# Queries and keys with the head ahead of the token: the layout between the projections and the score products

## The chip, the cores and the metric

The kernel runs on one core of a Trainium2 chip. The core has five engines with an instruction queue each: PE (TensorE, matrix products), DVE (VectorE), ACT (ScalarE), POOL (GpSimd) and SP (SyncE, which issues most of the DMAs here). Each engine works through its queue in order and waits at semaphores for the others. The metric is device time in microseconds (us) from one execution of the whole program; a single core runs, so it is that core's time. The time before is the median of three executions.

## What is computed

The reference is one pre-norm transformer layer in fp32 for 2048 tokens of width 1024. Its attention is not over the sequence: for every token, the 32 heads attend to each other.

```python
def _L0_attn_ref(hidden_states, wq, bq, wk, bk, wv, bv, wl, bl):
    ...
    q = (hidden_states @ wq.T + bq).reshape(B, S, H, D)
    k = (hidden_states @ wk.T + bk).reshape(B, S, H, D)
    v = (hidden_states @ wv.T + bv).reshape(B, S, H, D)
    ...
    scores = jnp.einsum('bshd,bstd->bsht', q, k) / np.sqrt(D).astype(np.float32)
    probs = jax.nn.softmax(scores, axis=-1)
    context = jnp.einsum('bsht,bstd->bshd', probs, v).reshape(B, S, E)
    return context
...
x = x + _L0_attn_ref(_layernorm(x, axis=-1), ...)
x = x + _L0_ffn_ref(_layernorm(x, axis=-1), ...)
```

H is 32 heads and D is 32 dimensions, so each token has a 32 x 32 score matrix. The feed-forward part is silu(x w1) * (x w2) times w3, with an inner width of 2752, where the three weights are first rounded to a 16-value code (NF4) with one scale for each block of 64.

## The kernel before

**Stages.** The kernel makes four passes one after the other. The query sweep, the key sweep and the value sweep each go over the 2048 tokens in 8 pairs of tiles; a tile is 128 tokens (P = 128), and a pair is put through a fast matrix product (`products`) with 7 block products in place of 8. Then comes the feed-forward part, which takes about two thirds of the time.

The query sweep normalises x, transposes it on PE for all three projections (`Inputs`), projects it to queries, brings them into their layout with `qk_T` and writes them to DRAM (`qD`). The key sweep loads the queries back (`ql`), projects the keys, brings them into the same layout with `qk_T` (`kd`), multiplies queries and keys (`scores`, in two parts of 64 products), takes the softmax (`softmax_T`) and writes the transposed probabilities to DRAM. The value sweep does the same with `v_T` and `context`, adds the residual and normalises again.

**Background.** Beside all of it, the feed-forward weights are quantised: for each block of 128 rows, ACT computes 15 steps `sg` (L211) and DVE folds each into `r` (L216). The code places these steps between the products by hand (`advance`, `flush`, `fill`). PE's order is exactly the one written; the order on the other engines is made by a scheduler when the program is built.

**The layout around the change.** A projected tile `c` holds 128 tokens on partitions and (head, dimension) along the free axis: `c[token, h*32 + d]`. For the score products, the dimension must be on partitions, since PE sums over partitions. DVE's transpose turns blocks of 32 x 32: for each group g of 32 tokens (partitions 32g to 32g+31) and each head it puts the dimension on the partition and the 32 tokens of the group along the free axis. Where these 32 tokens are written is a choice of the output's access pattern. Before, the tile `t` is (dimension; token, head): the 32 elements of a token, one for each head, lie next to each other, and a transpose writes every 32nd element.

The score product of token s in group g is a 32 x 32 x 32 product: its stationary operand is `qd[r, s, :]`, its moving operand `kd[r, s, :]`, with r the 32 partitions of group g. The four groups g use four row groups of PE's array, and the token's number modulo 4 selects the column group. [...]

`at` is the one score buffer in PSUM (four banks, `bufs=1`). The two DVE instructions that read it are the maximum (L543) and the subtraction (L545) in `softmax_T`.

**Lines that the steps touch.** L311 is the projection's matmul (`mm4`); L329 copies partial sums (g, s, u) on ACT, L346, L350 and L356 add them on DVE into the halves of the tiles `ce` and `co`, and L353 copies the last one into `ce`; L369 is the transpose in `qk_T`, L376 the one in `v_T`; L382 adds the bias; L390 is the score product; L543 to L557 are the softmax, with the exponential on ACT (L551) and the transpose of the probabilities (L557), which reads and writes consecutively; L522, L586 and L567 are the DMAs of queries and probabilities; L929 is the down projection of the feed-forward part.

Of the kernel before, what the change touches and what calls it, by code (L numbers as in the profile page):

```python
# [14 lines left out]
ALU = mybir.AluOpType  # L15
# [3 lines left out]
P = 128  # L19
# [3 lines left out]
D = 32  # L23
# [35 lines left out]
def preln_block_kernel(  # L59
# [14 lines left out]
    nc = tc.nc  # L74
# [291 lines left out]

    def qk_T(t, c, b):

        nc.vector.transpose(  # L369
            t.rearrange("p s h -> p h s"), c.rearrange("p (h d) -> p h d", d=D)  # L370
        )
        add_bias(t, b)

    def v_T(t, c, b):

        nc.vector.transpose(  # L376
            t.rearrange("p m d -> p d m"), c.rearrange("p (t d) -> p d t", d=D)
        )
        add_bias(t, b)

    def add_bias(t, b):
        nc.vector.tensor_tensor(t, t, b.unsqueeze(1).to_broadcast([P, 32, 32]), ALU.add)  # L382

    def scores(at, qd, kd, part):

        for s in range(16 * part, 16 * part + 16):
            c, s4 = s % 4, s // 4
            for g in range(4):
                r = slice(g * 32, (g + 1) * 32)
                nc.tensor.matmul(  # L390
                    at[c * 32 : (c + 1) * 32, g, s4 * 32 : (s4 + 1) * 32],
                    qd[r, s, :],
                    kd[r, s, :],
                    start=True,
                    stop=True,
                )
# [102 lines left out]
    for p in range(NP):  # L499
        more = p + 1 < NP  # L500
        now = nxt
        if more:
            load_x(2 * p + 2)
            load_x(2 * p + 3)
            nxt = Inputs(p + 1)

        def fill(n):
            if n in (7, 3):
                flush(1)
            if n == 5 and more:  # L510
                nxt.transposes(0)
                nxt.transposes(1)
            advance(0 if n == 5 else 1)

        cs = products(now.A, fill, (lambda name: None) if more else next_W("k"))
        flush(1)
        if more:
            nxt.finished()
        for j in range(2):
            t = work.tile([P, 32, NH], FP, tag="qd", name="qd", bufs=2)  # L520
            qk_T(t, cs[j], qb_sb)
            nc.sync.dma_start(qD[2 * p + j], t)  # L522
        now.finished_v()
        weight_chunk("kv"[p // 4], p % 4)
        advance(2)
        if p == NP - 2:
            first = load_A(opD, 0)
# [33 lines left out]
    def attend(i, qd, kd):  # L561

        at = ps_at.tile([P, 4, 512], FP, tag="at", name="sc")
        scores(at, qd, kd, 0)
        yield
        scores(at, qd, kd, 1)
        nc.sync.dma_start(pD[i], softmax_T(at))  # L567
        yield
# [13 lines left out]
    def load_tiles(src, p, tag, bufs):  # L582
        ts_ = []
        for j in range(2):
            t = work.tile([P, 32, NH], FP, tag=tag, name=tag, bufs=bufs)
            nc.sync.dma_start(t, src[2 * p + j])  # L586
            ts_.append(t)
        return ts_

    A = first  # L590
    for p in range(NP):
        nextA = load_A(opD, p + 1) if p + 1 < NP else load_A(opV, 0)
        qd = load_tiles(qD, p, "ql", 3)

        def fill(n):
            if n in (7, 2, 5, 4):
                part()
            advance(1)
            if n in (3, 5):
                flush(1)  # L600

        cs = products(A, fill, (lambda name: None) if p + 1 < NP else next_W("v"))
        flush(1)
        for j in range(2):
            t = work.tile([P, 32, NH], FP, tag="kd", name="kd", bufs=3)
            qk_T(t, cs[j], kb_sb)
            parts.append(attend(2 * p + j, qd[j], t))
        advance(2)
        A = nextA
# [70 lines left out]
    for p in range(NP):  # L680
# [26 lines left out]
        for j in range(2):  # L707
            t = work.tile([P, 32, D], FP, tag="vd", name="vd", bufs=3)
            v_T(t, cs[j], vb_sb)
            parts.append(gather(2 * p + j, pl[j], t))  # L710
# [320 lines left out]
```

## Time and profile before

| what | value |
|---|---|
| median of three executions | 2572.02 us (2563.67 to 2575.69) |
| the profiled execution | 2561.21 us, its span 2559.4 us |
| PE busy in the span | 2438.9 us (95%) |
| DVE busy | 2020.1 us (79%) |
| ACT busy | 1673.7 us (65%) |
| mean granted clock of PE | 0.985 of full speed |
| L369, transposes of queries and keys | 32, some 1.94 to 1.99 us each |
| L390, score products | 4096 matmul records, 42.2 us busy; 4096 weight loads, 38.0 us busy |

How to read it: a busy share is an average over stages with different limits, so the prediction reads each stage by itself. PE's matmuls overlap in its pipeline; a busy PE is not PE at its peak. PEld is PE's weight load, which overlaps its matmuls. The granted clock falls below 1.0 after PE has been idle for some time. In a list of waits, the name after the arrow is the instruction that released the waiting one, and "issue" means that the profile does not show what the engine waited for. A row of a group gives line, engine, operation, output and inputs, the shape and the count, then the busy time in us and the mean of one in ns, then the idle time before it.

### The profile page before, as it was taken

How to read it: one execution, taken by the hardware profiler on the slowest of the kernel's cores; microseconds unless marked ns; L12 is line 12 of the kernel's file. 1: busy time of each engine (PE TensorE's matmuls, PEld its weight loads, DVE VectorE, ACT ScalarE, POOL GpSimd, SP SyncE). 2: the span in 40 equal slices, each digit the busy share in tenths (PEclk: the TensorE clock that was granted, in tenths of full speed). 3: DMA queues.
4: the chain of work that ended last, by engine and by line, in shares of the span. 5: the costliest groups of instructions: out<-in, count | busy, mean ns of one | idle time of the engine just before them, and what ended most of it. 6: DMA issues, size and time to landing. Idle time of an engine off the chain costs nothing.

```text
span 2559.4 us, 36651 instructions
## 1 busy us (share of the span) xinstructions
PE 2438.9 (95%) x14160; PEld 1134.1 (44%) x14160; DVE 2020.1 (79%) x2240; ACT 1673.7 (65%) x3190; POOL 31.7 (1%) x72
## 2 busy tenths in 40 slices
PE   8899899999998999999999999999999999999998
PEld 4444444444444444444444444444444444444433
DVE  8999798888998588888888888889888897871222
ACT  4656554444654478979888898888987978861000
POOL 1000000000000000000000000000000000000000
PEclk9999999999999999999999999999999999999999
DMA  8778543656668673354644547335365253641474
GB/s 301 286 281 335 210 162 121 233 189 221 224 218 290 218 271 144 136 212 138 263 155 135 198 149 265 149 118 215 128 251 192 107 205 136 234 176 70 142 279 150
DMA packets 156848, 506.03 MB, mean 198 GB/s; under 512 B 13632, under 2 KB 67904, under 8 KB 136832
## 3 DMA queue, kind: packets, MB, share of 16 engines
q1 hardware_dynamic: 156096, 503.63, 54.3%
q8 instruction: 111, 1.82, 0.3%
q14 instruction: 65, 0.53, 0.1%
q10 hardware_dynamic: 576, 0.05, 0.0%
HBM read 317.77 MB, written 185.86 MB: 197 GB/s over the span
## 4 chain that ended last, share of the span: by engine, by line
PE 22%; DVE 21%; ACT 18%; issue 6%; DMA 1%; DVEq 0%; SPq 0%
DVE r L216 17%; PE z L311 9%; PE po L929 7%; ACT sg L211 7%; ACT wn L172 6%; PE q L311 3%; ACT r L172 3%; PE rr L311 2%; ACT wop L147 1%; DVE acc L950 1%; DMA acc<-x1d 1%; PE po L941 1%; DVE r L214 1%; DVE r L227 1%; PE ptw L146 0%
## 5 line engine op out<-in xcount | busy, mean ns | idle before, releaser
L211 ACT ACTIVATE sg<-wn 128x1024 f32<-128x1024 f32 (+1 forms) x975 | 1011.0, 1047 | 318.9 <-DVE r L216 272.4
L216 DVE SCALAR_TENSOR_TENSOR r<-sg,r 128x1024 f32<-128x1024 f32 (+1 forms) x910 | 1103.1, 1212 | 111.9 <-ACT sg L211 73.9
L929 PE MATMUL po<-w,h 128*128 128x512 f32 x1344 | 595.1, 597 | 17.0 <-DVE acc L950 13.8
L929 PEld LDWEIGHTS po<-w,h 128*128 128x128 f32 x1344 | 250.0, 190 | 336.5 <-issue 286.8
L311 PE MATMUL z<-xB,w 128*128 128x512 f32 x720 | 322.7, 597 | 13.7 <-DMA w<-wd 11.3
L311 PE MATMUL z<-xT,w 128*128 128x512 f32 x656 | 297.2, 596 | 2.0 <-ACT u L861 1.9
L311 PE MATMUL q<-xT,w 128*128 128x512 f32 x656 | 291.0, 592 | 0.0
L172 ACT ACTIVATE wn<-wn,rc 128x64 f32<-128x64 f32 x1032 | 270.1, 335 | 26.4 <-DVE rc L192 26.4
L311 PEld LDWEIGHTS z<-xB,w 128*128 128x128 f32 x720 | 134.5, 191 | 174.5 <-issue 164.3
L311 PE MATMUL z<-wB,A 128*128 128x512 f32 x384 | 188.6, 637 | 22.4 <-ACT u L329 22.4
L950 DVE TENSOR_TENSOR acc<-acc,po 128x512 f32<-128x512 f32 x192 | 129.7, 681 | 101.6 <-PE po L929 58.4
L311 PEld LDWEIGHTS q<-xT,w 128*128 128x128 f32 x656 | 123.6, 190 | 151.4 <-issue 149.5
L311 PE MATMUL z<-wT,A 128*128 128x512 f32 x384 | 181.3, 616 | 8.4 <-ACT u L329 6.4
L311 PEld LDWEIGHTS z<-xT,w 128*128 128x128 f32 x656 | 122.9, 191 | 149.8 <-issue 140.7
L311 PE MATMUL q<-wT,A 128*128 128x512 f32 x384 | 173.1, 593 | 3.0 <-DVE A L364 2.0
L172 ACT ACTIVATE r<-r,am 128x64 f32<-128x64 f32 x608 | 152.4, 338 | 27.9 <-DVE r L216 27.8
L311 PE MATMUL rr<-xB,w 128*128 128x512 f32 x328 | 150.0, 600 | 0.0
L184 DVE TENSOR_REDUCE am<-wn 128x16 f32<-128x1024 f32 (+1 forms) x65 | 78.3, 1204 | 59.4 <-ACT r L172 55.5
L311 PEld LDWEIGHTS z<-wB,A 128*128 128x128 f32 x384 | 75.0, 205 | 106.5 <-issue 79.3
L311 PEld LDWEIGHTS z<-wT,A 128*128 128x128 f32 x384 | 72.1, 195 | 91.0 <-issue 81.2
L311 PEld LDWEIGHTS q<-wT,A 128*128 128x128 f32 x384 | 71.8, 190 | 90.9 <-issue 84.2
L861 ACT COPY u<-z 128x512 f32<-128x512 f32 x41 | 23.5, 573 | 131.6 <-PE z L311 131.6
(104 smaller groups left out, 1798.4 us busy)
## 6 DMA issues: line engine op xcount, KB each, us to landing
w<-wd SPq DMA_DIRECT2D x41, 1280.0 KB, 6.9
acc<-x1d SPq DMA_DIRECT2D x96, 512.0 KB, 3.8
wd<-wop SPq DMA_DIRECT2D x21, 2048.0 KB, 7.0
x1d<-acc SPq DMA_DIRECT2D x80, 512.0 KB, 2.9
wn<-in_w_dram SPq DMA_DIRECT2D x63, 512.0 KB, 4.0
w<-wd SPq DMA_DIRECT2D x62, 512.0 KB, 4.1
xT<-xdT SPq DMA_DIRECT2D x28, 1024.0 KB, 7.2
xB<-xdB SPq DMA_DIRECT2D x24, 1024.0 KB, 5.2
```

The costliest lines, as they stand in the source:

```text
L147: nc.scalar.copy(o[:q, first + half], pt[:q])
L172: nc.scalar.mul(dst[:, ts(n, BLOCK)], src[:, ts(n, BLOCK)], by[:, n : n + 1])
L184: nc.vector.tensor_reduce(am[:, :nb], v.rearrange("p (b e) -> p b e", e=BLOCK), AX.X, ALU.max, apply_absolute_value=True,)
L211: nc.scalar.activation(t, v, AF.Copy, bias=EDGES[i], scale=BIG)
L214: nc.vector.tensor_scalar(r, t, code, -1.0, ALU.min, ALU.max)
L216: nc.vector.scalar_tensor_tensor(r, t, code, r, ALU.min, ALU.max)
L227: nc.vector.tensor_tensor(r3, r3, f, ALU.mult)
L311: nc.tensor.matmul(dst, w[:, k, :], xop[:, k, :], start=start and k == 0, stop=stop and k == 3, skip_group_check=True,)
L861: nc.scalar.copy(u2, self.z)
L929: nc.tensor.matmul(po, hs[c][j][:, ts(q, P)], w3T[c][:, ts(n, 512)], start=(c == g[0]), stop=(c == g[-1]), skip_group_check=True,)
L941: nc.tensor.matmul(po, hs[NFULL][r, ts(q, P)], w3T[NFULL][r, ts(n, 512)], start=False, stop=True, skip_group_check=True,)
L950: nc.vector.tensor_tensor(a[:, ts(n, 512)], a[:, ts(n, 512)], po, ALU.add)
```

## The change

Queries and keys are held as (dimension; head, token) in place of (dimension; token, head). The transposes of `qk_T` write the tile consecutively; the bias, one value for each head and dimension, is repeated along the last axis (the tokens) in place of the middle one; and the score products take token s as every 32nd element of the tile, in both operands. `add_bias` is now written out in its two places. The values' path keeps its layout, and the DMAs to and from DRAM move whole tiles as they did.

```diff
     def qk_T(t, c, b):

-        nc.vector.transpose(
-            t.rearrange("p s h -> p h s"), c.rearrange("p (h d) -> p h d", d=D)
-        )
-        add_bias(t, b)
+        nc.vector.transpose(t, c.rearrange("p (h d) -> p h d", d=D))
+        nc.vector.tensor_tensor(t, t, b.unsqueeze(2).to_broadcast([P, 32, 32]), ALU.add)

     def v_T(t, c, b):

         nc.vector.transpose(
             t.rearrange("p m d -> p d m"), c.rearrange("p (t d) -> p d t", d=D)
         )
-        add_bias(t, b)
-
-    def add_bias(t, b):
         nc.vector.tensor_tensor(t, t, b.unsqueeze(1).to_broadcast([P, 32, 32]), ALU.add)

     def scores(at, qd, kd, part):
...
                 nc.tensor.matmul(
                     at[c * 32 : (c + 1) * 32, g, s4 * 32 : (s4 + 1) * 32],
-                    qd[r, s, :],
-                    kd[r, s, :],
+                    qd[r, :, s],
+                    kd[r, :, s],
                     start=True,
                     stop=True,
                 )
```

## The prediction

> **What bounds the kernel now.** I read the busy time of the engines in four stretches first (query sweep after its start, key sweep, value sweep, feed-forward part; below I also call them stretches):
>
> ```profile
> core 0: us, PE busy (x) PEld busy (x) DVE busy (x) ACT busy (x) POOL busy (x), PEclk, DMA share, GB/s
> 35.00:283.00 248.00, 228.18 (x612) 106.79 (x611) 232.22 (x288) 164.05 (x333) 14.95 (x24) 0.97 0.78 291
> 283.00:553.00 270.00, 250.22 (x4582) 126.94 (x4581) 227.08 (x222) 126.73 (x244) 0.00 (x0) 0.97 0.47 175
> 553.00:850.00 297.00, 269.13 (x4715) 141.62 (x4714) 257.94 (x276) 150.44 (x295) 12.72 (x32) 0.96 0.71 236
> 850.00:2559.00 1709.00, 1666.30 (x4183) 744.48 (x4181) 1279.29 (x1426) 1223.62 (x2302) 0.00 (x0) 0.99 0.49 178
> ```
>
> Columns: stretch, its length, busy us of each engine, granted clock, DMA. The change touches the first two rows only. In the last, PE works 1666 of 1709 us, so whatever the sweeps gain or lose reaches the end almost whole. In the first, DVE is the fuller engine (232 of 248), in the second PE (250 of 270). Next, who waited for whom. PE and DVE in the query stretch:
>
> ```profile
> PE z L311 <- ACT u L329: 15.1, 7, 3.3
> PE pt L440 <- DVE xn L306: 3.7, 2, 2.8
> PE q L311 <- DVE co L356: 0.9, 2, 0.5
> ...
> DVE xn L306 <- POOL rs L108: 5.5, 10, 0.7
> DVE am L184 <- ACT r L172: 2.8, 1, 2.8
> ```
>
> and in the key stretch:
>
> ```profile
> PE sc L390 <- issue: 14.2, 5, 4.4
> PE sc L390 <- DVE kd L382: 5.6, 1, 5.6
> ...
> DVE ce L346 <- PE r L311: 17.7, 4, 5.3
> DVE mx L543 <- PE sc L390: 4.1, 6, 1.5
> ```
>
> Columns: total us, times, longest. In the query stretch DVE never waits for PE; PE waits for ACT's copy u, and ACT for DVE (36 waits of sg for r, 45.3 us): DVE sets the pace. In the key stretch each waits for the other. The timeline tells what stands behind "issue":
>
> ```profile
> 434.92 1.22 DVE L545 TENSOR_TENSOR pr<-sc,mx 128x1024 f32<-128x1024 f32 x1
> ...
> 436.24 1.41 PE L390 MATMUL sc<-kd,ql 32*32 32x32 f32 x128 [4.44 <-issue]
> ```
>
> (start, us, what.) The score products of the next tile begin when DVE has finished reading the last tile's scores out of the one score buffer: PE waits for DVE's queue.
>
> **The change, part by part.** Comparing the two builds, no instruction changes its place on any engine, the DMAs are the same whole tiles, and the queue of SP is untouched. Three things change their cost.
>
> *1. The transposes (L369).* These are the rows of the key stretch:
>
> ```profile
> L557 DVE STREAM_TRANSPOSE prT<-pr 128x1024 f32<-128x1024 f32 x16 | 19.8, 1240 | 0.3
> L555 DVE TENSOR_TENSOR pr<-pr,sm 128x1024 f32<-128x1024 f32 x16 | 19.5, 1218 | 0.3
> ...
> L382 DVE TENSOR_TENSOR kd<-kd,kb 128x1024 f32<-128x1024 f32 x16 | 19.2, 1203 | 0.1
> L369 DVE STREAM_TRANSPOSE kd<-ce 128x1024 f32<-128x1024 f32 x8 | 15.5, 1938 | 2.0 <-ACT ce L353 2.0
> ```
>
> L557 reads and writes consecutively, 1.240 us; L369 reads consecutively and writes every 32nd element, 1.938 us (1.98 in the query sweep). After the change L369 has L557's form: 16 x (1.98 - 1.24) = 11.8 us less DVE work in the query sweep, 16 x (1.938 - 1.240) = 11.2 in the key sweep.
>
> *2. The bias additions.* The bias is now repeated along the last axis, as the factor sm is in L555: 1.218 against 1.203 us, 32 x 0.015 = 0.5 us more. Nothing beside part 1.
>
> *3. The score products (L390).* Both operands, the stationary and the moving one, are now read every 32nd element. No PE row of the trace reads so; this is the open price. A half tile is 128 passes in 1.29 us:
>
> ```profile
> 426.88 1.29 PE L390 MATMUL sc<-kd,ql 32*32 32x32 f32 x128
> ...
> 428.10 3.70 PE L311 MATMUL z<-wT,A 128*128 128x512 f32 x8
> ```
>
> They run on four row groups of the array at once, so a group has 32 passes, 1290 / 32 = 40 ns each. L311 streams 512 elements in 429 ns (3.43 us for 8 in the undisturbed stretches), 0.84 ns per element, so 27 of the 40 ns are the 32 elements. There are 32 half tiles, so 32 x 32 = 1024 passes stand one behind the other: each ns on a pass is 1.02 us of PE.
> Low end: PE reads at any step for nothing, 0. High end: every element of load and stream costs the 1.938 us / 1024 = 1.89 ns of the strided transpose, and load and stream of a pass take turns: 2 x 32 x 1.89 = 121 ns in place of 27, +96 us. I take the nearest row, what the step adds per element on DVE: (1.938 - 1.240) us / 1024 = 0.68 ns, 32 x 0.68 = 22 ns on a pass, the weight load hidden beside the stream as now (PEld is busy half of PE's time): 22 ns x 1024 = +22 us of PE, a half tile of 2.0 us.
> The row of L369 against L557 shows that memory touched with a wide step costs more. [...]
>
> *The sum.* Query sweep: DVE sets the pace, so of 11.8 us most arrives; PE's own waits after the start are 15.1 + 3.7 + 0.9 = 19.7 us, enough room. As PE is 228 of 248 busy, it becomes the next bound at some places: I take two thirds, -8 (ends 0 and -15, the latter with half of the 3% of clock that idle PE lost, 7 us). Key sweep: PE has six waits, 19.8 us. Between a place where DVE waited for PE and such a wait stand about two transposes, so each shrinks by 1.4, the smallest (1.1) vanishes: -8 (ends 0 and -11). PE pays +22. The waits that are left, some 12 us, absorb little of this: DVE's own four long waits are for PE (17.7 us), so a late PE makes DVE late too; I take 3. Key sweep: 22 - 8 - 3 = +11. The value sweep's work is the same. Together -8 + 11 = +3 us.
>
> The profiled execution took 2561.2 us (span 2559.4 and 1.8 around it): it would become 2564. The median of the three runs shown is 2572.0, 10.8 above it (0.4%); the forecast in its terms is 2575.
>
> **Rivals.**
> *A. PE reads every 32nd element for nothing.* For: on PE fp32 asks for an element only each 0.84 ns, and four row groups already share the time of a pass, 13 of its 40 ns being no streaming. Against: the one engine whose step can be compared paid 56%. Then -8 - 8, and some 2 us of clock that is no longer lost to idle stretches: -18, 2554.
> [...]
> *C. The transposes don't get faster* because L557 owes its 1.24 us to its input rather than its order of writing: then only PE's part is left, 22 - 3 = +19, 2591. Against: L376 reads with a step as well and costs the same as L369, so the write decides.
>
> **How the numbers follow.** Forecast 0.38, A 0.27, B 0.30, C 0.05. What a measurement of this kernel can tell from no change is about 0.5%, 13 us. The forecast's own range is 2562 to 2592 (22 us of PE moved by 10 either way and 5 of the savings): a quarter of it lies beyond 2585, a twentieth below 2559. A is beyond 13 us in three cases of four, B nearly always, C in half. Faster 0.27 x 0.75 + 0.38 x 0.05 = 0.22; slower 0.30 x 0.95 + 0.38 x 0.25 + 0.05 x 0.5 = 0.40; same 0.38. The range goes from A's place, 2552, to a little above B's, 2628; the full high end (+96 us of PE) is left out.
>
> **What would show it.** L369 at 1.24 us, 32 times. [...] PE's waits in the query stretch fall from 19.7 to about 12 us, and the key sweep begins about 8 us earlier. [...] I am wrong if the half tile stays at 1.29 or passes 2.3 us, if the query stretch doesn't shorten with its transposes, or if the value sweep or the feed-forward part changes its length by more than 5 us, for nothing is changed there.

## The result, and the profile after

The changed kernel takes 2559.16 us in the median of 20 executions (2551.48 to 2564.3), the kernel before 2569.34 us in 20 (2560.44 to 2578.13). The ratio is 0.9961 with a 95% interval of 0.9951 to 0.9970: 10 us faster, where the forecast was 3 us slower.

The profiled execution of the changed kernel took 2564.3 us, the slowest of its 20; the profiled execution of before, 2561.2 us, lies below all but one of the 20 above. The two traces therefore show what the single steps did, but not the difference in time. These are the four stretches of the changed kernel, with the same columns and limits as before:

```profile
35.00:283.00 248.00, 231.32 (x737) 108.99 (x737) 229.17 (x295) 172.55 (x358) 14.94 (x24) 0.98 0.81 304
283.00:553.00 270.00, 264.44 (x4487) 141.70 (x4479) 216.32 (x220) 124.13 (x227) 0.00 (x0) 0.98 0.45 167
553.00:850.00 297.00, 267.40 (x4712) 140.81 (x4711) 253.97 (x272) 147.24 (x292) 12.67 (x32) 0.96 0.70 236
850.00:2559.00 1709.00, 1667.47 (x4176) 745.33 (x4174) 1279.19 (x1425) 1223.39 (x2302) 0.00 (x0) 0.99 0.49 177
```

In the key stretch PE is now busy 264 of 270 us instead of 250, and DVE 216 instead of 227. The limits are those of the kernel before; the key sweep now begins ahead of 283 us, so its first wait lies outside this row and more of the value sweep inside. Between the first and the last score product PE is busy 250.4 of 256.0 us, where it was 236.9 of 251.0. The groups of the changed lines (line, engine, operation, output and inputs, shape, count, then busy us, mean ns, and the idle time before):

```profile
L385 PE MATMUL sc<-kd,ql 32*32 32x32 f32 x4096 | 57.7, 263 | 11.1 <-DMA ql<-qD 5.6 <-issue 4.6 <-PE z L311 0.9
L385 PEld LDWEIGHTS sc<-kd,ql 32*32 32x32 f32 x4096 | 53.8, 168 | 35.8 <-issue 34.1 <-PE z L311 1.7
...
L369 DVE STREAM_TRANSPOSE kd<-ce 128x1024 f32<-128x1024 f32 x8 | 10.0, 1249 | 2.6 <-ACT ce L353 2.6
L369 DVE STREAM_TRANSPOSE kd<-co 128x1024 f32<-128x1024 f32 x8 | 10.0, 1244 | 0.1
L369 DVE STREAM_TRANSPOSE qd<-ce 128x1024 f32<-128x1024 f32 x8 | 9.9, 1240 | 1.4 <-ACT ce L353 1.4
L369 DVE STREAM_TRANSPOSE qd<-co 128x1024 f32<-128x1024 f32 x8 | 9.9, 1236 | 0.0
```

This is the group of the score products in the kernel before:

```profile
L390 PE MATMUL sc<-kd,ql 32*32 32x32 f32 x4096 | 42.2, 204 | 19.8 <-issue 14.2 <-DVE kd L382 5.6
```

The score products are now L385, and the bias additions of queries and keys L370. The transposes came down to 1.24 us, and the score products' matmuls went from 42.2 to 57.7 us of busy time. Both sides of the trade are there. On the timeline a call of `scores` shows the price for one half tile, 1.80 us in place of the 1.29 shown ahead of the prediction:

```profile
413.30 1.80 PE L385 MATMUL sc<-kd,ql 32*32 32x32 f32 x128
```

PE's idle time in front of score products fell from 19.8 to 11.1 us. And PE's waits in the query stretch, which were 15.1, 3.7 and 0.9 us:

```profile
PE z L311 <- ACT u L329: 8.4, 6, 1.9
PE pt L435 <- DVE xn L306: 2.6, 1, 2.6
```

They are now 11.0 us in place of 19.7: PE waits 8.7 us less in the query sweep.

### The profile page after: what moved, and what is told of

Read it like the earlier page. It is cut to its first block, busy times and chain, and to the rows that moved or that the text cites. A ratio compares the mean times of both kernels' runs of the same rounds, so it can differ in the third digit from the quotient of the medians.

```text
span 2562.5 us, 36651 instructions
## 1 busy us (share of the span) xinstructions
PE 2456.5 (96%) x14160; PEld 1151.3 (45%) x14160; DVE 2001.2 (78%) x2240; ACT 1674.9 (65%) x3190; POOL 31.6 (1%) x72
## 4 chain that ended last, share of the span: by engine, by line
PE 24%; DVE 20%; ACT 17%; issue 6%; DMA 1%; DVEq 0%; SPq 0%
DVE r L216 16%; PE z L311 9%; PE po L924 9%; ACT sg L211 7%; ACT wn L172 5%; PE q L311 3%; ACT r L172 3%; PE rr L311 2%; ACT wop L147 1%; DVE acc L945 1%; PE po L936 1%; PE ptw L146 1%; DVE r L214 1%; DVE r L227 0%; ACT u L856 0%
## 5 line engine op out<-in xcount | busy, mean ns | idle before, releaser
L216 DVE SCALAR_TENSOR_TENSOR r<-sg,r 128x1024 f32<-128x1024 f32 (+1 forms) x910 | 1104.2, 1213 | 113.5 <-ACT sg L211 75.5
L311 PE MATMUL z<-xB,w 128*128 128x512 f32 x720 | 323.3, 598 | 14.3 <-DMA w<-wd 12.0
L311 PE MATMUL z<-xT,w 128*128 128x512 f32 x656 | 297.2, 596 | 2.0 <-ACT u L856 1.9
L311 PE MATMUL q<-xT,w 128*128 128x512 f32 x656 | 291.0, 592 | 0.0
L311 PEld LDWEIGHTS z<-xB,w 128*128 128x128 f32 x720 | 134.9, 192 | 175.4 <-issue 165.0
L311 PE MATMUL z<-wB,A 128*128 128x512 f32 x384 | 186.3, 631 | 17.5 <-ACT u L329 17.3
L311 PEld LDWEIGHTS q<-xT,w 128*128 128x128 f32 x656 | 123.7, 190 | 151.3 <-issue 149.4
L311 PEld LDWEIGHTS z<-xT,w 128*128 128x128 f32 x656 | 123.0, 191 | 149.7 <-issue 140.6
L311 PE MATMUL z<-wT,A 128*128 128x512 f32 x384 | 181.4, 617 | 7.1 <-ACT u L329 4.5
L311 PE MATMUL q<-wT,A 128*128 128x512 f32 x384 | 173.1, 593 | 2.4 <-DVE A L364 1.5
L311 PE MATMUL rr<-xB,w 128*128 128x512 f32 x328 | 150.0, 601 | 0.0
L311 PEld LDWEIGHTS z<-wB,A 128*128 128x128 f32 x384 | 73.6, 201 | 100.9 <-issue 78.3
L311 PEld LDWEIGHTS z<-wT,A 128*128 128x128 f32 x384 | 72.4, 195 | 89.9 <-issue 81.7
L311 PEld LDWEIGHTS q<-wT,A 128*128 128x128 f32 x384 | 71.9, 190 | 90.0 <-issue 82.9
```

Of the source, the lines that this page charges most:

```text
L216: nc.vector.scalar_tensor_tensor(r, t, code, r, ALU.min, ALU.max)
L311: nc.tensor.matmul(dst, w[:, k, :], xop[:, k, :], start=start and k == 0, stop=stop and k == 3, skip_group_check=True,)
```

## The experiments

"Ratio" is always the time against the kernel before, run on the same chip beside it. "Half tile" is the 128 matmul records of one call of `scores`, two for each of its 64 products (4096 records in the profile for the kernel's 2048 products). The two theories that the first four runs were to tell apart concern PE's price (who pays for the step: the stationary operand, the moving one, or both) and where it ends up (on the path that sets the end, or hidden in PE's waits).

**1. The reading alone.** From the kernel before, only the operands change; the scores then mix heads and tokens.

```diff
-                    qd[r, s, :],
-                    kd[r, s, :],
+                    qd[r, :, s],
+                    kd[r, :, s],
```

> Layout and transposes as before, but the score products read both operands every 32nd element, so the scores mix heads and tokens. This is the price of the reading alone: a half tile of 1.79 us in place of 1.29, 32 x 0.50 = 16 us of PE. Theory of the critical path (PE sets the pace of the key sweep where it doesn't wait for DVE): +11 to +16 us (ratio 1.004 to 1.006), all in the key sweep. Rival (the extra PE time falls into PE's 20 us of waits in the key sweep and is hidden): 0 to +4 us (ratio 1.000 to 1.0015).

Measured: 2578.05 us, ratio 1.0025 (1.0013 to 1.0036), between the two theories. The group of the score products shows why:

```profile
L390 PE MATMUL sc<-kd,ql 32*32 32x32 f32 x4096 | 57.2, 263 | 12.8 <-issue 7.1 <-DMA ql<-qD 5.7
```

The busy time rose by 57.2 - 42.2 = 15.0 us, but the idle time in front of these products fell from 19.8 to 12.8. By this pair of traces 7.0 us of the price went into waits and 8.0 us lengthened the key sweep; against the second trace of before (run 10), whose idle time is 18.0 us, it is 5.2 and 9.9. The ratio gives 6.4 us (3.3 to 9.3). A price that arrives whole lies outside this interval, and so does full cover (a ratio of 1.000), while the upper end that the rival allowed itself (1.0015) lies just inside.

**2. The writing alone.** From the changed kernel, the operands are read as before; again the scores mix heads and tokens.

```diff
-                    qd[r, :, s],
-                    kd[r, :, s],
+                    qd[r, s, :],
+                    kd[r, s, :],
```

> Transposes write consecutively as in the changed kernel, but the score products read consecutive elements as before, so the scores mix heads and tokens. This is the gain of the writing alone: 23 us less DVE work. A half tile of 1.29 us. If the sum is additive with the reading alone and the whole change: -10 - 14 = about -24 us (ratio 0.9905 to 0.992): query sweep -11, key sweep -8 and more. Rival (DVE's gain counts in the query sweep alone, where DVE sets the pace): -11 us (ratio 0.996).

Measured: 2551.43 us, ratio 0.9921 (0.9906 to 0.9936), -20 us, some 4 us less than the additive sum. The rival's time (DVE counts in the query sweep alone, 0.996) lies outside the interval.

```profile
L385 PE MATMUL sc<-kd,ql 32*32 32x32 f32 x4096 | 42.2, 203 | 16.1 <-issue 10.1 <-DMA ql<-qD 6.0
L385 PEld LDWEIGHTS sc<-kd,ql 32*32 32x32 f32 x4096 | 37.9, 104 | 41.3 <-issue 40.8
```

With DVE faster and PE's price absent, the idle time in front of the score products is 16.1 us. Between this kernel and the changed one lies the reading alone: 15.5 us of price, of which 16.1 - 11.1 = 5.0 fall into waits, so 10.5 should arrive. The ratios differ by 0.0040, which is 10.3 us; that the two are so close is luck, since the intervals leave some 6 to 15 us. The reading alone and the writing alone add up to +6.4 - 20.3 = -14, against the measured -10 of both together. This is within the intervals, and on the side to be expected, as there is less waiting left for the price to fall into. The trace of the writing alone shows only a part of its -20 us: some 9 us at the first score product (282.5 us, against 291.1 and 291.8 in the two traces of before), and 1 to 3 us between the first and the last (247.7 us, against 251.0 and 248.6). Where the other 9 us sit, it doesn't show, so that they are DVE's gain in the key sweep is not shown either.

**3 and 4. One operand at a time.** The queries are the stationary operand, the keys the moving one, and each has its own layout. In the first run only the queries take the new one:

```diff
+    def old_T(t, c, b):
+
+        nc.vector.transpose(
+            t.rearrange("p s h -> p h s"), c.rearrange("p (h d) -> p h d", d=D)
+        )
+        nc.vector.tensor_tensor(t, t, b.unsqueeze(1).to_broadcast([P, 32, 32]), ALU.add)
...
-            qk_T(t, cs[j], kb_sb)
+            old_T(t, cs[j], kb_sb)
...
                     qd[r, :, s],
-                    kd[r, :, s],
+                    kd[r, s, :],
```

> Only the queries get the new layout: their transposes write consecutively and the stationary operand is read every 32nd element; the keys keep the old layout. Theory S (the moving operand's step costs, the weight load hides beside it): a half tile of score products stays at about 1.29 us, the query sweep gains about 11 us, the time is 11 us below the kernel before (ratio 0.996), as good as the whole change or better. Theory L (the stationary operand's step costs): a half tile of about 1.79 us, +16 us of PE in the key sweep, query sweep still -11, in sum near 0 (ratio 0.999 to 1.001). Theory B (each operand costs its half): a half tile of about 1.54 us, -11 + 6 = -5 us (ratio 0.998).

In the second only the keys (the queries use `old_T`, and the operands are `qd[r, s, :]` and `kd[r, :, s]`):

> Only the keys get the new layout: their transposes write consecutively and the moving operand is read every 32nd element; the queries keep the old layout. Theory S (the moving step costs): a half tile of about 1.79 us; the query sweep is unchanged, the key sweep gets +16 us of PE and -11 us of DVE, of which some 8 arrive: +5 to +8 us (ratio 1.002 to 1.003). Theory L (the stationary step costs): 1.29 us, -8 us (ratio 0.997). Theory B (half each): 1.54 us, about 0 (ratio 0.999 to 1.001).

Measured: queries alone 2559.88 us, ratio 0.9957 (0.9941 to 0.9972); keys alone 2565.69 us, ratio 0.9982 (0.9971 to 0.9993). The score products of the queries alone, and of the keys alone:

```profile
L392 PE MATMUL sc<-kd,ql 32*32 32x32 f32 x4096 | 50.2, 233 | 14.8 <-issue 9.6 <-DMA ql<-qD 5.3
L392 PEld LDWEIGHTS sc<-kd,ql 32*32 32x32 f32 x4096 | 46.4, 145 | 39.5 <-issue 33.4 <-DVE kd L377 6.1
```

```profile
L392 PE MATMUL sc<-kd,ql 32*32 32x32 f32 x4096 | 47.5, 229 | 14.9 <-issue 9.1 <-DMA ql<-qD 5.8
L392 PEld LDWEIGHTS sc<-kd,ql 32*32 32x32 f32 x4096 | 42.0, 104 | 40.3 <-issue 39.6
```

The stationary operand's step costs 50.2 - 42.2 = 8.0 us of PE, the moving one's 5.3; both together cost 15.0 to 15.5. So theory B is right on PE's side: each pays, and a weight load with a step isn't hidden beside the stream. The loads' mean, 105 ns before, grew to 145 ns with the queries alone and stayed at 104 with the keys alone. Both of its times were missed: -11 us for the queries alone, where it had -5, and -4.6 for the keys alone, where it had about 0. The price was again partly covered, as the idle time fell by 5.0 us with the queries alone and by 4.9 with the keys alone; in the latter DVE's faster transposes have a part in this.

**5 and 6. How far the step may go.** The kernel before with both operands read every 4th and every 2nd element of a smaller window (again a mix of heads and tokens):

```diff
+        q4, k4 = (
+            t.rearrange("p s h -> p (s h)").rearrange("p (b x k) -> p b x k", x=32, k=4)
+            for t in (qd, kd)
+        )
...
-                    qd[r, s, :],
-                    kd[r, s, :],
+                    q4[r, s // 4, :, s % 4],
+                    k4[r, s // 4, :, s % 4],
```

> The kernel before, but both operands of the score products are read every 4th element (a step of 16 bytes) out of a window of 128 elements, so the scores mix heads and tokens. It asks what the step costs, not the time. [...] Rival (it is the distance of 128 bytes, or the spread over 4 KB, that costs): near 1.29 us (busy 42 to 46 us).

> [...] Rival (any step but one costs the whole price): about 1.78 us (busy 57 us).

The groups with every 4th element, and with every 2nd:

```profile
L394 PE MATMUL sc<-kd,ql 32*32 32x32 f32 x4096 | 50.2, 239 | 17.6 <-issue 12.5 <-DMA ql<-qD 5.1
```

```profile
L394 PE MATMUL sc<-kd,ql 32*32 32x32 f32 x4096 | 42.6, 205 | 22.0 <-issue 16.6 <-DMA ql<-qD 5.4
```

Every 2nd element costs almost nothing (42.6 against 42.2 us), every 4th 8.0 us, every 32nd 15.0. So the price sets in between a step of 8 and one of 16 bytes; a step of 12 bytes was not run. Both rivals miss: the 50.2 us of every 4th element lie above the 42 to 46 of the one, the 42.6 of every 2nd far below the 57 of the other. About half of the price at 128 bytes comes on top of that at 16; these two runs don't show what from.

These two traces, one execution each (2572.45 and 2568.24 us, beside 2570.5 for the kernel before), also limit what was read from the first four. From the first to the last score product they took 258.4 us (every 4th) and 257.2 us (every 2nd, without a price), as long as the reading alone, 258.2, while the two traces of before took 251.0 and 248.6. The queries alone and run 8 below, which differ only in the value sweep's code, took 253.6 and 260.7. And of the 8.0 us of every 4th element only 2.2 fell into waits (19.8 to 17.6). So how a price divides between waits and path can't be read from one trace closer than by some us; the ratios of the first two runs are the firmer evidence.

**7. A padded tile.** The changed kernel with 36 elements for each head in place of 32:

```diff
-            t = work.tile([P, 32, NH], FP, tag="qd", name="qd", bufs=2)
+            t = work.tile([P, 32, 36], FP, tag="qd", name="qd", bufs=2)
+            nc.gpsimd.memset(t[:, :, 32:], 0.0)
...
-            t = work.tile([P, 32, NH], FP, tag="kd", name="kd", bufs=3)
+            t = work.tile([P, 32, 36], FP, tag="kd", name="kd", bufs=3)
```

(`qD` and the loaded tile `ql` likewise; `qk_T` works on the first 32 of each 36.)

> [...] POOL sets the four spare elements of the queries to zero, since whole tiles go to DRAM; the DMAs move an eighth more. The score products read every 36th element. [...] Rival (the distance alone costs): 1.79 us, 57 us busy, ratio 0.996 or worse by the padding's own work.

```profile
L386 PE MATMUL sc<-kd,ql 32*32 32x32 f32 x4096 | 50.5, 240 | 14.9 <-DMA ql<-qD 7.4 <-issue 7.4
```

A step of 144 bytes costs 8.3 us, about as one of 16 bytes does (8.0), and not the 15.5 of 128 bytes. So it isn't the distance: the longer step is the cheaper one, and why 128 bytes cost more, no run shows. The time, 2561.6 us and a ratio of 0.9965 (0.9953 to 0.9977), did not follow the lower price; it is where the rival had it. The first score products began at 284.9 us, some 4 us later than in the unpadded traces (281.6 and 279.2). But in the second padded kernel below, whose query sweep is the same code, they began at 280.9, so this delay is not a fixed price of the padding. Inside the key sweep the 7 us are missing too: from the first to the last score product the two padded traces took 254.2 and 254.4 us, the unpadded ones 256.0 and 253.9. In this time PE's products into z (L311) took 121.3 and 121.7 us in place of 118.3 and 116.6, at a granted clock of 0.96 in place of 0.98 and 0.99, and PE waited 7.4 and 7.2 us in place of 5.5 and 5.3. In the trace of before, after PE's 4.44 us of idle time that end at 436.24 us, the clock was 0.71 from 436 to 438 us, 0.50 to 440, 0.94 to 442 and 1.00 to 444; why it was lower in the padded traces, no run here shows.

**8 and 9. Towards a faster kernel.** The queries alone, and in the value sweep the context products' operands exchanged, so that the transpose of the context writes consecutively:

```diff
-                        prT[r, m, :],
                         vd[r, m, :],
+                        prT[r, m, :],
...
-            cx.rearrange("p (h d) -> p d h", d=D),
-            at[:, :, 0:256].rearrange("p c (s d) -> p d s c", d=D),
+            cx.rearrange("p (h d) -> p h d", d=D),
+            at[:, :, 0:256].rearrange("p c (s h) -> p h s c", h=NH),
```

> Only the queries get the new layout, and in the value sweep the two operands of the context products change places: the values become stationary, the probabilities moving, both still read consecutively. The context then lies as (dimension; head) in the score buffer, and the transpose that brings it back (16 of 1.97 us) writes consecutively: 16 x 0.73 = 11.7 us less DVE work in the value sweep, at no price on PE (a half tile of context products stays at 1.29 us). Theory (PE's waits for ACT's copies in the value sweep, 13.7 us, come from DVE's queue): another -5 to -10 us beside the -11 of the queries alone: ratio 0.992 to 0.994. Rival (the value sweep is set by PE, DMA and the loads of the feed-forward part): no more than the queries alone, 0.9957.

```profile
L406 PE MATMUL cx<-pl,vd x4096: 184/191/255, 558.2 to 825.7; 32*32 32x32 f32 x196
L622 DVE STREAM_TRANSPOSE cx<-cx x16: 1240/1244/1251, 566.8 to 826.5; 128x1024 f32<-128x1024 f32 x16
```

(Count, then the shortest, median and longest in ns, first and last start.) The transposes fell from a median of 1974 ns in the kernel before to 1244 at no price on PE, whose median stayed at 191 ns. From the last score product to the last context product this run took 287.3 us, against 292.0 with the queries alone. The time is 2556.33 us, ratio 0.9945 (0.9931 to 0.9959): some 3 us below the queries alone and not the 5 to 10 expected, and the intervals overlap. The same exchange on the padded kernel:

> The padded kernel, and the context products' operands changed over as in the run with the queries alone: 11.7 us less DVE work in the value sweep. There this gave the stretch from the end of the score products to the end of the context products 287.3 us in place of 292. Theory: -4 to -5 us beside the padded kernel (ratio 0.992 to 0.993 if the padding helps, 0.994 to 0.995 if not). Rival (the value sweep's gain is lost again in the feed-forward part): the padded kernel's ratio.

2558.59 us, ratio 0.9954 (0.9942 to 0.9967): 3 us again, below what was expected, with overlapping intervals. The queries alone with the exchanged operands have the lowest ratio of all kernels that leave the scores unmixed, though against the changed kernel it isn't clear of the measurement.

**10 and 11. Second traces.** Both kernels unchanged:

> The kernel before, unchanged, for a second trace: it tells how far the places of the sweeps differ from one execution to the next. The first score products of the first trace began at 291.1 us and the last at 542.1 us. Theory (the sweeps repeat within 2 us, and what differs between executions is the feed-forward part): 290 to 293 and 541 to 545 us. Rival (the first trace was a lucky one from the start): both later by 4 us or more.

> The changed kernel, unchanged, for a second trace: the first score products began at 281.6 us in the first one, the last ended at 537.9. Theory (the query sweep gains all of its 11.8 us of DVE work, less about 2): begin at 280 to 283 us, end at 534 to 540 us.

In the second trace of before the score products ran from 291.8 to 540.4 us, where expected for the start and 0.6 us before it for the end. In the second one of the changed kernel they ran from 279.2 to 533.1, each about 1 us before what was expected. These lines give the first and last start in the first trace of before and in the two of the changed kernel:

```profile
L390 PE MATMUL sc<-kd,ql x4096: 184/209/258, 291.1 to 542.1; 32*32 32x32 f32 x196
```

```profile
L385 PE MATMUL sc<-kd,ql x4096: 208/263/323, 281.6 to 537.6; 32*32 32x32 f32 x196
```

```profile
L385 PE MATMUL sc<-kd,ql x4096: 209/263/323, 279.2 to 533.1; 32*32 32x32 f32 x196
```

The four traces with the new layout for the queries and no padding or exchange (both traces of the changed kernel, the queries alone, the writing alone) begin at 281.6, 279.2, 281.1 and 282.5 us, mean 281.1. Six without it (both of before, the keys alone, the reading alone, every 4th, every 2nd) begin at 291.1, 291.8, 292.0, 292.7, 291.7 and 291.4, mean 291.8. The query sweep's gain is 10.7 us. (The queries alone with the exchanged operands, whose query sweep is the same code as that of the queries alone, began at 277.7; with it the gain would be 11.4.)

## Why the prediction was wrong

The forecast was -8 for the query sweep, +22 on PE for the reading, -8 and -3 in the key sweep; in sum +3, while the kernel became 10 us faster. Its structure held: two costs that lie in different sweeps, DVE setting the pace of the first. The step that failed by most is PE's price: +22 us, from a row of DVE and with the weight load hidden, where +15.5 was measured and the load's step is not hidden. Two smaller terms were also put too far towards slower (the query sweep by 2.7 us, what the waits absorb by some 2), and one the other way (DVE's gain in the key sweep, by 4.3). With these the sum is -4; where the other 6 us of the measured -10 sit stays open.

*The transposes* were right: 1.24 to 1.25 us against the 1.24 forecast, and the additions 1.21 to 1.23 us. (L376, which reads and writes with a step, took 1.97 and 1.99 us in the trace of before.)

*The query sweep:* I took two thirds of DVE's 11.8 us, "as PE ... becomes the next bound at some places". Measured: 10.7 us, nine tenths. PE had waited 19.7 us there, DVE never for PE, and the profile gave no row for the third that I withheld: after the change PE still waits 11.0 us there.

*PE's price:* the step added 0.47 ns per element (15.5 us over 1024 passes of 32), not DVE's 0.68: a half tile of about 1.79 us in place of my 2.0, +15.5 instead of +22. The row taken was of another engine and of a write, and this size failed. The overlap failed besides: I had the load "hidden beside the stream as now", while the stationary operand alone costs 8.0 us, more than the moving one's 5.3. Rival A, which needed 1.29 us for a half tile, falls. That load and stream take turns, from which rival B has its chance of 0.30 and the range its upper end of 2628 us, no run shows; the runs showed prices for the two operands that about add up (8.0 and 5.3 alone, 15.0 to 15.5 together), and a half tile below the 2.3 us that the prediction set as a bound (1.29 us and 32 us more over 32 half tiles, 13 us beyond the savings of 8 + 8 + 3). The change's own price lies between A's and mine.

*What the waits absorb:* I let the remaining waits absorb 3 of 22 us, because "a late PE makes DVE late too". With the reading alone the ratio lets 3.3 to 9.3 of 15.0 us arrive, so more than that vanished. Between the writing alone and the change the traces give 5.0 of 15.5, which is the case that the sum needed: 2 us more than mine, and not clear of the differences between traces. The two longest of DVE's waits for PE in the key sweep of the changed kernel are:

```profile
DVE ce L346 <- PE r L311: 24.8, 5, 7.0
...
DVE mx L538 <- PE sc L385: 7.3, 6, 2.4
```

My reason was right in the second line: the maximum that reads the score buffer waited 7.3 us for PE in place of 4.1, also with the reading alone (7.3), and 4.0 with the writing alone. The first line, 17.7 before, doesn't show it, since it is 21.8 with the writing alone, where PE pays nothing. The timeline suggests why more than 3 us vanished all the same: the wait for the one score buffer that is shown ahead of the prediction ends with DVE's subtraction (434.92 us), and a quantising step (L216, 433.79 us) stands just ahead of it in DVE's queue. PE's extra time may fall into such waits first; no run isolates this.

*The key sweep's gain from DVE* was over-estimated: with the writing alone PE's idle time before score products fell by 3.7 us (19.8 to 16.1), where I had 8. From busy and idle time of the score products, the key sweep's change is +15.5 - 8.7 = +6.8 us, where I had +11. With -10.7 that makes -4 us at the end of the key sweep. In the traces, the last score products start 542.1 and 540.4 us after the start before the change, and 537.6 and 533.1 us after it: 5.9 us earlier in the mean. The key sweep itself, from the first to the last score product, grew by 5.2 us, from 251.0 and 248.6 to 256.0 and 253.9; beside the 6.8 above, PE's products into z (L311) took 1.7 us less in it.

What stays open is where the rest of the 10 us sits. In the traces the part behind the last score product even took longer after the change: 2024.9 and 2026.5 us, against 2017.3 and 2022.2 before. By itself neither the value sweep (some 2 us longer in the mean, to the last context product) nor the feed-forward part (some 4 us) passes the 5 us that the prediction set as a sign of being wrong. The second trace of before (2564.4 us) also lies below the median of its kernel, and both traces of the changed kernel (2564.3 and 2561.4 us) above theirs, so that the traced ends do not differ in the mean. The single executions of before spread over 18 us. Neither part was changed, and no run here shows a cause there.

A slip of the prediction's own: 10 us of price and 5 of savings around 2575 give a range of 2560 to 2590, not 2562 to 2592. The chances hardly move by it.

## What to carry to other kernels

When a layout moves cost from one engine to another, ask in which stage each engine sets the pace: here 12 us of DVE work left a sweep that DVE bound, and nearly all of it arrived, while the 15 us that PE took on landed in a sweep where PE still had waits, and by the ratios a third to somewhat over a half of it vanished, with wide intervals. Before giving a number to what a wait absorbs of added work, look at what its releaser does in the meantime; here that number could not be had closer than by some us. A step on PE's operands cost 13 to 37% of these small products' busy time where it cost anything, and not a factor; the row of another engine, taken for its price, came out too high by 6.5 of 22 us.

## What the runs showed of the hardware

All on 32 x 32 x 32 products in fp32 with their operands on four groups of 32 partitions; many run at once (before, 4096 matmul records of 204 ns in the mean in 42.2 us of busy time). Busy us of the 4096 records:

| step of the operands | matmul busy us |
|---|---|
| 1 element, both | 42.2 |
| 2 elements (8 bytes), both | 42.6 |
| 4 elements (16 bytes), both | 50.2 |
| 32 elements (128 bytes), both | 57.2 to 57.7 |
| 36 elements (144 bytes), both | 50.5 and 50.6 |
| 32 elements, stationary alone | 50.2 and 50.5 |
| 32 elements, moving alone | 47.5 |

I had not expected that a step of 128 bytes costs nearly twice as much as one of 144 (15.0 to 15.5 us on top, against 8.3), nor that the weight load's step costs more than the stream's (8.0 against 5.3).
